# Contexts of later batches turned by VectorE and kept turned in DRAM, in a fused cross-attention and expert kernel

## The chip, the cores and the metric

The kernel runs on one core of a Trainium2 chip. A core has five engines with queues of their own: TensorE (PE in the profile; its weight loads are shown apart as PEld), VectorE (DVE), ScalarE (ACT), GpSimd (POOL) and SyncE (SP), which here only issues transfers. The time is device microseconds of one execution, and the median over runs counts.

## The reference

Two layers follow each other, all in float32. The first is a gated cross-attention: `x` (4 batches, 256 rows, 512 columns) gives the queries, `ctx_4096` (4 batches, 1601 rows, 512 columns) the keys and values. There are 32 query heads of 128 columns, 8 key and value heads, so that four query heads share one. The second is a router with low-rank experts.

```python
q = (query @ Wq + bq).reshape(B, L, NKV, G, HDIM)
k_, v_ = jnp.split(kv @ Wkv + bkv, 2, axis=-1)
...
scores = jnp.einsum('blkgd,bmkd->bkglm', q, k) * scale
attn = jax.nn.softmax(scores, axis=-1)
o = jnp.einsum('bkglm,bmkd->blkgd', attn, v).reshape(B, L, NHEAD * HDIM)
...
x = x + jnp.tanh(g_xattn[0]) * attention(layernorm(x), ctx_4096, ...)
x = x + jnp.tanh(g_ffn[0]) * experts(layernorm(x), ...)
```

## The kernel before

**Groups.** Batch b, key head h and half l of the 256 query rows make a group; there are 64, in this order. In group sc_h_l of a batch `run_group` interleaves the score matmuls of the group (L1142, tiles `sc`) with the value products of the group before it (L1233, tiles `av`). Scores are copied to `p` by ACT (L1151), their maximum is folded by DVE as they come (L1067 to L1073), spread over the partitions by a short chain that ends with a transpose of 32x32 blocks into `mb` (L1086 to L1107, then L1100), and then subtracted from `p` tile by tile (L1181, DVE), exponentiated (L1184, ACT), and summed (again L1067 to L1073, tiles `sm`). `p` is a ring of buffers: a score tile of a later group waits for the sum of the tile that held its buffer.

**Filler.** The rest of PE's work is cut into tasks and put between the groups and between the steps of a group: query, key and value projections of coming heads (L896 for keys and queries, L907 for values), the output projection (L1310), and the turning of contexts.

**Contexts.** A batch's context is needed with its 512 columns on the partitions (`ctxT`, 4 chunks of 128 columns by 1602 places), as an operand of the projections. It comes in 13 tiles of 128 rows, the last of 65. `ctx_steps` loads a tile into one of two `stage` buffers; `turn_ctx` has PE turn it by four transposes (L258, tile `pt_ctx`), which ACT copies out of PSUM (L260). For batch 0 half of the copies are DVE's. For batches 1 to 3 all this is a task of one step to a tile, which runs in group sc_6_1 of the batch before, once the last value projection of that batch (V pair 3) has used the old context: there is one `ctxT`.

**Projections by seven products.** Keys, values and queries are computed two heads at a time with seven products in place of eight, from blocks of the operands: the context as two column halves by two row halves (b11, b12, b21, b22), and sums of them. The sums of the context are T1 = b12 - b11, T2 = b22 - T1, T4 = b21 - T2 (`ctx_sums`, L723, tile `T`), done here for each pair of tiles by pieces of 128 columns, and, once all are done, b12 := b22 - b12 in place in `ctxT` (`last_sums`, L734, in two pieces of 417 and 384 columns, then L738 for the 65 remaining rows). The products of a pair run in the order 1 (b11), 2 (b21), 6 (T2), 7 (b12), 5 (T1), 4 (T4), 3 (b22), by column pieces of 417 and 384. Product 7 needs the b12 of L734. ACT copies and DVE adds (L941, L951) bring the products into `kT`.

**At a boundary of batches.** The order is: V pair 3 of the old batch; group sc_6_1 with the turning; group sc_7_0; then K pair 0 of the new batch (tiles `pxk`, `pzk`, `pyk`), whose first step is `last_sums`; and after it V pair 0 and group sc_7_1. Weights for the next pairs are loaded and summed ahead, and kept in DRAM for the other batches.

**Order of the work.** The order of PE, DVE and ACT is that in which the program issues it; the program holds a clock of its own for each engine. `later` puts a piece of DVE or ACT work in a named queue with its planned length and the time or the key that it needs, `pump` issues from the queue whose head can start first, and `force(key)` issues what is needed until the key is done. A plan's LAG is the time from a load's issue at which the piece that needs it may be planned. The order of SP and POOL is the scheduler's. Each engine works strictly in its order, and a transfer issued from SP waits in SP's queue for what it needs.

Of the kernel before, what the change touches and what calls it, by code (L numbers as in the profile page):

```python
# [10 lines left out]
F32 = mybir.dt.float32  # L11
# [4 lines left out]
P = 128  # L16
# [11 lines left out]
def flamingo_kernel(  # L28
# [93 lines left out]
    clock = {"now": 0.0, "v": 0.0, "a": 0.0, "hold": 0.0}  # L122
    free = [0.0] * NBANK
    done = {}
    queues = {q: deque() for q in ("sub", "oT", "so", "exp", "ln", "T", "norm", "sum", "low", "low_a")}

    def vec(ns, ready=None):

# [41 lines left out]
    def force(key):  # L170


        while key not in done:
            q = next((q for q in queues.values() if any(p[4] == key for p in q)), None)
            if q is None:

                assert pump(most=1), key
                continue
            ready = q[0][2]
            if not isinstance(ready, float):  # L180
                force(ready)

            engine, start = q[0][0], start_of(q[0])
            for name, other in queues.items():
                fit = 1200 if name == "sub" else FIT
                while other is not q and other and other[0][0] == engine:
                    if start_of(other[0]) + other[0][1] > start + fit:
                        break
                    take(other)
            take(q)  # L190
        return done[key]
# [390 lines left out]
        xa_t[b] = pool.tile([P, NL, D], F32, tag=f"xa{b}", name=f"xa_{b}", bufs=1)  # L582
    STAGE = 2

    LAG_DMA, LAG_CTX, LAG_X = 2500, 1700, 3000


    JOINT = 2
# [60 lines left out]
    def ctx_col(i):  # L649

        half, t = divmod(i, HK // P)
        return half * HW + HT + t * P
# [5 lines left out]
    def new_ctx(b):  # L658
        ctxT_t[b] = pool.tile([P, NC, 2 * HW], F32, tag="ctxT", name=f"ctxT_{b}", bufs=1)
        rest_t[b] = pool.tile([P, NC, REST], F32, tag="rest", name=f"rest_{b}", bufs=1)  # L660
        if REST0 < HT:

            nc.gpsimd.memset(ctxT_t[b][:, :, REST0:HT], 0.0)

    def ctx_steps(b):

        staged = {}

        def load(n):
            i = ctx_order[n]  # L670
            s = pool.tile([P, D], F32, tag="stage", name=f"ctx_{b}_{i}", bufs=STAGE)
            nc.sync.dma_start(s[: rows[i]], ctx_kv[b, i * P : i * P + rows[i], :])
            staged[i] = s

        def begin():
            new_ctx(b)
            new_sums(b)

        def step(n):
            def run():  # L680
                i = ctx_order[n]
                if n + STAGE - 1 < KT:
                    load(n + STAGE - 1)
                turn_ctx(b, i, staged.pop(i))
                if n % 2 == 1 and i < FULL:
                    ctx_sums(b, ctx_col(i) - HW, P)
                if i == FULL:
                    ctx_sums(b, 0, HT)
                if n == KT - 1:
                    done["ctx", b] = clock["now"] + 1000  # L690
            return NC * TR_COST, LAG_CTX, run, True

        def first():
            for n in range(STAGE - 1):
                load(n)


        return [(0, 0, first), (0, ("pair", "v", b - 1, NKV // 2 - 1), begin)] + [
            step(n) for n in range(KT)
        ]  # L700

    def new_sums(b):
        t = pool.tile([P, 6 * HW + 2 * REST], F32, tag="T", name=f"T_{b}", bufs=1)
        T_t[b] = (
            t[:, : 6 * HW].rearrange("p (n c k) -> p n c k", n=3, c=2),
            t[:, 6 * HW :].rearrange("p (c k) -> p c k", c=2),
        )

    def ctx_sums(b, s0, n):


        ct, T = ctxT_t[b], T_t[b][0]
        lo, hi = slice(s0, s0 + n), slice(HW + s0, HW + s0 + n)
        b11, b12, b21, b22 = ct[:, 0:2, lo], ct[:, 0:2, hi], ct[:, 2:4, lo], ct[:, 2:4, hi]
        t1, t2, t4 = T[:, 0, :, lo], T[:, 1, :, lo], T[:, 2, :, lo]
        for out_, x_, y_ in (
            (t1, b12, b11),
            (t2, b22, t1),
            (t4, b21, t2),
        ):  # L720
            later(
                "T", "v", 80 + 2.3 * n, clock["now"] + 1000.0,
                lambda o=out_, x=x_, y=y_: nc.vector.tensor_tensor(o, x, y, ALU.subtract),  # L723
            )

# [16 lines left out]
    def turn_ctx(b, i, src):  # L742
        if i < FULL:
            lo = ctx_col(i)
            transpose_rows(
                src, P, ctxT_t[b][:, :, lo : lo + P], f"ctx_{b}_{i}", b > 0 or i % 2 == 1
            )
            return

        rest = rest_t[b]  # L750
        transpose_rows(src, REST, rest, f"ctx_{b}_{i}", True)
        nc.scalar.copy(ctxT_t[b][:, :, :REST0], rest[:, :, :REST0])
        act(300)
        nc.scalar.copy(ctxT_t[b][:, :, HW : HW + HT], rest[:, :, REST0:])
        act(300)
# [925 lines left out]
    def run_group(cur, prev, ahead=AHEAD, most=NC * TR_COST):  # L1681


        for j in range(NPAIR + ahead):
            if cur is not None and j < NPAIR:
                score_unit(cur, j)
                if j == NPAIR - 1 and cur[0] == B - 1 and cur[1] >= NKV - 2:
                    softmax(cur)
                short_tasks(most)
            if prev is not None and prev[2] == 0 and j > 2:  # L1690
                block_sums(prev, j >= NPAIR - 1)
            if prev is not None and j >= ahead:
                av_unit(prev, j - ahead)
                short_tasks(most)
        if cur is not None and not (cur[0] == B - 1 and cur[1] >= NKV - 2):
            softmax(cur)
# [173 lines left out]
    for hi, (b, h) in enumerate(heads):  # L1870
        pair, coming = (b, h // 2), next_pair(b, h // 2)
        nxt = heads[hi + 1] if hi + 1 < len(heads) else None
        for l in range(NL):
            now = hi * NL + l
            cur = (b, h, l)
            if cur == last:
                break
            if (h, l) == (NKV - 5, 1) and b + 1 < B and (b + 1) % JOINT == 0:
                load_pair("q", b + 1, 0)
                tasks.append(Task(x_steps(b + 1), now + 7))  # L1880
            run_group(cur, prev)
            if prev is not None:
                steps = out_steps(prev)
                if steps:
                    tasks.insert(0, Task(steps, now + 1 if by_blocks(*prev[:2]) else None))
                    if by_blocks(*prev[:2]):
                        out_task[prev[:2]] = tasks[0]
            prev = cur
            if (b, h, l) == (B - 1, NKV - 3, NL - 1):
                flush(lambda t: t in out_task.values())  # L1890
                tail_space()
                tasks.append(Task(ffn_weight_steps() + [(0, 0, early_norms)]))
                both = [ffn_steps(*t) for t in early]
                tasks[:0] = [Task(route, now + 4) for route, _ in both]
                tasks.extend(Task(steps, spare=True) for _, steps in both)
            if nxt is not None and nxt[0] % JOINT == 0:
                tasks.append(Task(q_steps(*nxt, l), now, first=True))
            elif nxt is not None and l == 0:
                load_q(*nxt)
            if coming is not None and (h % 2, l) == (0, 1):  # L1900
                cb, cp = coming
                if cb == b:
                    then = lambda c=coming: next_weights("v", *c)
                    steps = sum(pair_steps("k", cb, cp, then), [])
                else:
                    steps = first_k_steps(cb)
                tasks.append(Task(steps, (hi | 1) * NL + (NL - 1) * (cb == b), now))
            if coming is not None and (h % 2, l) == (1, 0):
                cb, cp = coming
                follow = next_pair(cb, cp)  # L1910
                then = None if follow is None else lambda f=follow: next_weights("k", *f)
                for part in pair_steps("v", cb, cp, then):
                    tasks.append(Task(part, (hi | 1) * NL + NL, now))
                if cb == b and cp == NKV // 2 - 1 and b + 1 < B:
                    tasks.append(Task(ctx_steps(b + 1)))
            if (h, l) == (NKV - 1, NL - 1) and b + 1 < B:

                force(("T", "kv", b + 1))
                force(("w", "v", b + 1, 0))
            window(now)  # L1920
            if l == NL - 1 and nxt == heads[-1]:
                load_wo(*nxt)
# [51 lines left out]
```

## Time and profile before

| what | value |
|---|---|
| median of 3 runs (lowest to highest) | 2558.49 us (2557.35 to 2559.09) |
| span of the profiled execution | 2555.5 us |
| granted TensorE clock | 1.00 of full speed throughout |
| PE busy on L1142 and L1233, scores and value products | 775.9 and 766.1 us |
| PE busy on `pt_ctx` (L258), 208 transposes, batch 0's among them | 273 ns median of one |
| ACT copies of `pt_ctx` (L260) to `ctxT`, 42 | 589 ns median of one |
| DVE subtraction L1181 (128x1024) and exponential L1184 | 1137 and 990 ns mean |
| DVE sums L723: 128x256, 128x66, 128x834, 128x768 | 54, 9, 3 and 3 of them |
| transfers | 167.16 MB, mean 65 GB/s |

The span is that of one execution of the program, taken by the hardware profiler; the runs' times hold some 3 us around it. A row of the profile's groups gives a line of the kernel, the engine, the operation with its output and input tiles, the number of instructions, and their time. In a timeline the columns are start, length, engine, line, operation, tiles and number. Matmuls are pipelined, so that the lengths of neighbouring PE rows overlap a little: the distance from start to start is what a row costs.

### The profile page before, as it was taken

To read this page: it belongs to the slowest core of one execution; us is meant where nothing else is said; L and a number is where in the kernel's file an instruction comes from. 1 tells how busy PE (TensorE), PEld (TensorE's weight loads), DVE (VectorE), ACT (ScalarE), POOL (GpSimd) and SP (SyncE) were. 2 spreads that over 40 slices of the span, in tenths; PEclk is the share of its full clock that TensorE was granted. 3 is DMA by queue.
4 is the path that set the end of the run, shared out by engine and by line. 5 is a ranking of instruction groups with operands and counts; after the bars stand their busy time and mean duration, and the time that the engine had idled before them with its cause. 6 is when DMAs were issued, how large, how long until landed. Compare 5 with 4: busy or idle time off the path is not lost.

```text
span 2555.5 us, 26175 instructions
## 1 busy us (share of the span) xinstructions
PE 2547.3 (100%) x9235; PEld 1487.8 (58%) x9235; DVE 2202.6 (86%) x3310; ACT 1188.1 (46%) x1897; POOL 150.4 (6%) x401
## 2 busy tenths in 40 slices
PE   9999999999999999999999999999999999999999
PEld 7557566565555656455565665756656455555554
DVE  4889898899889989899788887878889899998897
ACT  3544454445434555455444444445454445544551
POOL 0000000000000000110000000000000000000000
PEclk9999999999999999999999999999999999999999
DMA  4313222324110111012121111212221011111000
GB/s 158 123 64 108 87 95 84 114 85 149 48 56 23 44 52 56 25 40 83 49 81 37 62 52 62 81 48 81 85 84 56 25 52 52 52 44 52 17 17 33
DMA packets 75499, 167.16 MB, mean 65 GB/s; under 512 B 5372, under 2 KB 32028, under 8 KB 72808
## 3 DMA queue, kind: packets, MB, share of 16 engines
q1 hardware_dynamic: 74424, 164.41, 19.3%
q8 instruction: 73, 1.20, 0.2%
q0 software_dynamic: 416, 0.81, 0.1%
q14 instruction: 58, 0.48, 0.1%
q10 hardware_dynamic: 528, 0.26, 0.0%
HBM read 119.06 MB, written 46.40 MB: 65 GB/s over the span
## 4 chain that ended last, share of the span: by engine, by line
PE 99%; DVE 1%; DMA 0%; ACT 0%; issue 0%; DVEq 0%; ACTq 0%
PE av L1233 28%; PE sc L1142 28%; PE pxk L896 6%; PE pxv L907 6%; PE pxq L896 4%; PE pyk L896 3%; PE pyv L907 3%; PE po L1310 3%; PE pox L484 3%; PE pyq L896 2%; PE pzk L896 2%; PE pzv L907 2%; PE poy L484 1%; PE pzq L896 1%; PE ptv L1020 1%; PE pk L803 1%
## 5 line engine op out<-in xcount | busy, mean ns | idle before, releaser
L1142 PE MATMUL sc<-qT,kT 128*128 128x512 f32 (+1 forms) x1664 | 775.9, 592 | 0.0
L1151 ACT COPY p<-sc 65x512 f32<-65x512 f32 x820 | 474.3, 586 | 636.5 <-PE sc L1142 575.2
L1233 PE MATMUL av<-p,v 65*128 65x512 f32 x1640 | 766.1, 592 | 1.2 <-ACT p L1184 1.2
L1233 PEld LDWEIGHTS av<-p,v 65*128 65x128 f32 x1640 | 309.5, 190 | 376.2 <-issue 370.8
L1142 PEld LDWEIGHTS sc<-qT,kT 128*128 128x128 f32 (+1 forms) x1664 | 307.0, 186 | 374.3 <-issue 340.4
L1181 DVE TENSOR_TENSOR p<-p,mb 65x512 f32<-65x512 f32 x442 | 485.9, 1137 | 0.1
L1184 ACT ACTIVATE p<-p 65x512 f32<-65x512 f32 x442 | 423.1, 990 | 38.6 <-DVE p L1181 34.5
L1073 DVE TENSOR_TENSOR mx<-mx,p 128x1024 f32<-128x1024 f32 x252 | 308.1, 1223 | 137.9 <-ACT p L1151 134.8
L1073 DVE TENSOR_TENSOR sm<-sm,p 128x1024 f32<-128x1024 f32 x252 | 307.4, 1220 | 9.8
L1090 POOL COPY quad_sm<-quad_sm 32x16 f32<-32x16 f32 x186 | 70.7, 380 | 2088.3 <-DVE quad_sm L1086 2083.1
L896 PE MATMUL pxq<-xq,wq 128*128 128x256 f32 x512 | 131.2, 379 | 0.0
L941 ACT ACTIVATE kT<-pxk,biasT 128x384 f32<-128x384 f32 (+1 forms) x120 | 57.9, 508 | 141.8 <-PE pxk L896 141.0
L896 PEld LDWEIGHTS pxq<-xq,wq 128*128 128x128 f32 x512 | 92.5, 189 | 31.2 <-issue 15.3
L941 ACT ACTIVATE qT<-pxq,biasT 128x256 f32<-128x256 f32 x64 | 30.3, 473 | 140.2 <-PE pxq L896 140.2
L944 ACT COPY v<-pxv 128x384 f32<-128x384 f32 x90 | 43.0, 477 | 104.8 <-PE pxv L907 104.8
L896 PE MATMUL pxk<-T,wk 128*128 128x417 f32 (+1 forms) x240 | 90.4, 499 | 0.0
L907 PE MATMUL pxv<-wv,T 128*128 128x128 f32 x720 | 90.2, 275 | 0.0
L896 PE MATMUL pxk<-ctxT,wk 128*128 128x417 f32 (+1 forms) x240 | 90.0, 499 | 0.0
L907 PE MATMUL pxv<-wv,ctxT 128*128 128x128 f32 x720 | 90.0, 275 | 0.0
L907 PEld LDWEIGHTS pxv<-wv,T 128*128 128x128 f32 x720 | 86.4, 192 | 4.7 <-issue 4.3
L907 PEld LDWEIGHTS pxv<-wv,ctxT 128*128 128x128 f32 x720 | 86.4, 192 | 4.7 <-issue 4.3
L1067 DVE TENSOR_TENSOR mx<-p,p 128x1024 f32<-128x1024 f32 x63 | 76.8, 1220 | 13.1 <-ACT p L1151 12.8
(264 smaller groups left out, 2809.6 us busy)
## 6 DMA issues: line engine op xcount, KB each, us to landing
wo<-in_L_xattn_Wo_dram SPq DMA_DIRECT2D x18, 1024.0 KB, 5.3
kept_q<-wq SPq DMA_DIRECT2D x16, 896.0 KB, 4.8
wq<-kept_q SPq DMA_DIRECT2D x16, 896.0 KB, 5.1
wo<-kept_wo SPq DMA_DIRECT2D x13, 1024.0 KB, 5.8
wk<-kept_k SPq DMA_DIRECT2D x11, 896.0 KB, 4.6
wv<-kept_v SPq DMA_DIRECT2D x11, 896.0 KB, 4.4
ctx<-in_ctx_dram SPq DMA_DIRECT2D x36, 256.0 KB, 2.7
wq<-in_L_xattn_Wq_dram SPq DMA_DIRECT2D x32, 256.0 KB, 3.1
```

The source lines that it names most:

```text
L484: nc.tensor.matmul(bk[:, :HD], left[i]()[:, c, :], blk[:, c, :], start=first and c == 0, stop=c == 1, skip_group_check=True,)
L896: nc.tensor.matmul(bk[:, :n], a(SLOT[i], c), operand(i, c, s, n), start=first and c == 0, stop=c == 1, skip_group_check=True,)
L907: nc.tensor.matmul(bk[:, t * HDIM : (t + 1) * HDIM], operand(i, c, s + t * P, P), a(SLOT[i], c), start=first and t == 0 and c == 0, stop=c ...
L941: nc.scalar.activation(dst, src, AF.Identity, bias=bias_of(kind, h0 + f))
L1067: nc.vector.tensor_tensor(acc, p[first], p[first + 1], op)
L1073: nc.vector.tensor_tensor(acc, acc, p[j], op)
L1142: nc.tensor.matmul(sc[:r, :], kT_t[b, h][:, key_col(i) : key_col(i) + r], qT_t[b, h][:, :, l * P : (l + 1) * P], start=True, stop=True,)
L1151: nc.scalar.copy(p[:r, k, :], sc[:r, :])
L1181: nc.vector.tensor_tensor(p, p, m, ALU.subtract)
L1184: nc.scalar.activation(p, p, AF.Exp, scale=scale)
L1233: nc.tensor.matmul(av, v_t[b, h][:r, i, :], p_t[key][j][:r, k, :], start=(j == 0 and k == 0), stop=(j == NPAIR - 1 and k == len(pairs[j]) ...
L1310: nc.tensor.matmul(po, oT_t[key][:, g, :], w_t["o", b, h][:, g, :], start=(g == 0), stop=(g == G - 1),)
```

## The change

**Turning.** `ctx_steps` no longer loads and turns. In each of the first twelve groups of batches 0 to 2, ahead of `run_group`, `swap_ctx` handles one tile of the next batch's context (two in the twelfth): SP loads it into a `stage` buffer; DVE transposes its 32x32 blocks (up to sixteen along the columns, for four bands of 32 rows) into the other `stage` buffer, as a piece of a new queue "turn"; SP stores each band of 32 rows, 64 KB, in a DRAM tile of 512 columns by 1602 places, in runs of 32 elements (128 bytes). A tile must be stored before the next one is begun. The last tile's row 1600 is left out of this. Only batch 0 is still turned by PE.

**Reloading.** When V pair 3 of the old batch is done, `begin` asks for the kept context to be complete, makes the new `ctxT`, and reloads it by eight transfers, four of 768 KB and four of 32 KB, and two for `rest`, the tile of the last 65 rows, all on SP. Row 1600 comes by two transfers of 512 single elements on POOL.

**Sums.** The T sums of the context are now six instructions, by the two column pieces of 417 and 384 instead of seven narrower pieces. They are planned 24 us (LAG_CTX) after the reload's issue, and so is `last_sums`, which is forced by K pair 0's first step as before. In the order that the program issues, the three sums of the first piece come among the maxima of group sc_7_0 (at the second boundary the third of them later), and those of the second piece and `last_sums` between and behind that group's subtractions L1181. At the first two boundaries the output projection `po_6_0` now stands ahead of the first K product on PE. PE has 39 rows of four transposes less, DVE 39 block transposes more and 45 sums fewer, ACT 36 copies of 128x512 fewer and those of the last tiles.

```diff
-    LAG_DMA, LAG_CTX, LAG_X = 2500, 1700, 3000
+    LAG_DMA, LAG_CTX, LAG_X = 2500, 24000, 3000
...
+    def swap_ctx(b, n):
+
+        i = ctx_order[n]
+        if n:
+            force(("kept", b, n - 1))
+        if b not in ctx_kept:
+            ctx_kept[b] = dram.tile([D, 2 * HW], F32, tag=f"ctx_{b}", name=f"kept_ctx_{b}")
+        kept_b = ctx_kept[b].rearrange("(j k) w -> k j w", k=32)
+        r = rows[i] // 32 * 32
+        src = pool.tile([P, D], F32, tag="stage", name=f"ctx_{b}_{i}", bufs=STAGE)
+        nc.sync.dma_start(src[:r], ctx_kv[b, i * P : i * P + r, :])
+        dst = pool.tile([P, D], F32, tag="stage", name=f"swap_{b}_{i}", bufs=STAGE)
+
+        def swap():
+            nc.vector.transpose(dst[:r], src[:r])
+
+        def store():
+            for a in range(r // 32):
+                if i < FULL:
+                    lo = ctx_col(i) + 32 * a
+                else:
+                    lo = HW * a
+                nc.sync.dma_start(
+                    kept_b[:, :, lo : lo + 32],
+                    dst[32 * a : 32 * a + 32].rearrange("k (j w) -> k j w", w=32),
+                )
+
+        later("turn", "v", 710, clock["now"] + LAG_DMA, swap, ("swap", b, n))
+        later("turn", "v", 0, ("swap", b, n), store, ("kept", b, n))
+
     def ctx_steps(b):
...
         def begin():
+            force(("kept", b, KT - 1))
             new_ctx(b)
             new_sums(b)
-
-        def step(n):
-            def run():
-                i = ctx_order[n]
-                if n + STAGE - 1 < KT:
-                    load(n + STAGE - 1)
-                turn_ctx(b, i, staged.pop(i))
-                if n % 2 == 1 and i < FULL:
-                    ctx_sums(b, ctx_col(i) - HW, P)
-                if i == FULL:
-                    ctx_sums(b, 0, HT)
-                if n == KT - 1:
-                    done["ctx", b] = clock["now"] + 1000
-            return NC * TR_COST, LAG_CTX, run, True
...
+            ends = [(0, HT, HW), (1, HT, HW), (0, 0, 32), (1, 0, 32)]
+            for c in range(0, NC, 2):
+                for half, lo, hi in ends:
+                    lo, hi = half * HW + lo, half * HW + hi
+                    nc.sync.dma_start(ct[:, c : c + 2, lo:hi], kept_b[:, c : c + 2, lo:hi])
+            for half in range(2):
+                nc.sync.dma_start(
+                    rest[:, :, 32 * half : 32 * half + 32], kept_b[:, :, HW * half : HW * half + 32]
+                )
+            one = ctx_kv[b, LK - 1, :].rearrange("(c p) -> p c", p=P)
+            nc.gpsimd.dma_start(rest[:, :, REST - 1], one)
+            nc.gpsimd.dma_start(ct[:, :, HW + HT - 1], one)
+            done["ctx", b] = clock["now"] + LAG_CTX
+            for s0, n in parts_of_half:
+                ctx_sums(b, s0, n, LAG_CTX)
+
+        return [(0, ("pair", "v", b - 1, NKV // 2 - 1), begin)]
...
-    def ctx_sums(b, s0, n):
+    def ctx_sums(b, s0, n, lag=1000.0):
...
-                "T", "v", 80 + 2.3 * n, clock["now"] + 1000.0,
+                "T", "v", 80 + 2.3 * n, clock["now"] + lag,
...
+            if b + 1 < B and now % (NKV * NL) < KT - 1:
+                for n in range(KT)[now % (NKV * NL) :][: 1 if now % (NKV * NL) < KT - 2 else 2]:
+                    swap_ctx(b + 1, n)
             run_group(cur, prev)
```

More of the change, by code (lines that the diff above doesn't have):

```diff
@@ L124, in flamingo_kernel @@
     done = {}
-    queues = {q: deque() for q in ("sub", "oT", "so", "exp", "ln", "T", "norm", "sum", "low", "low_a")}
+    queues = {q: deque() for q in ("sub", "oT", "so", "exp", "ln", "T", "norm", "sum", "turn", "low", "low_a")}
     def vec(ns, ready=None):
@@ L663, in new_ctx @@
             nc.gpsimd.memset(ctxT_t[b][:, :, REST0:HT], 0.0)
-    def ctx_steps(b):
-        staged = {}
-        def load(n):
-            i = ctx_order[n]
-            s = pool.tile([P, D], F32, tag="stage", name=f"ctx_{b}_{i}", bufs=STAGE)
-            nc.sync.dma_start(s[: rows[i]], ctx_kv[b, i * P : i * P + rows[i], :])
-            staged[i] = s
+    ctx_kept = {}
+    def swap_ctx(b, n):
[23 more added lines that the diff above has]
+        later("turn", "v", 0, ("swap", b, n), store, ("kept", b, n))
@@ L675, in begin @@
+    def ctx_steps(b):
         def begin():
+            force(("kept", b, KT - 1))
             new_ctx(b)
             new_sums(b)
-        def step(n):
-            def run():
-                i = ctx_order[n]
-                if n + STAGE - 1 < KT:
-                    load(n + STAGE - 1)
-                turn_ctx(b, i, staged.pop(i))
-                if n % 2 == 1 and i < FULL:
-                    ctx_sums(b, ctx_col(i) - HW, P)
-                if i == FULL:
-                    ctx_sums(b, 0, HT)
-                if n == KT - 1:
-                    done["ctx", b] = clock["now"] + 1000
-            return NC * TR_COST, LAG_CTX, run, True
@@ L693, in first @@
[L693 to L700, printed above, removed]
+            ct, rest = ctxT_t[b], rest_t[b]
+            kept_b = ctx_kept[b].rearrange("(c p) w -> p c w", p=P)
+            spare = rows[FULL] % 32
+            whole = rows[FULL] - spare
+            assert spare == 1 and whole == 64 and REST0 == 32
+            ends = [(0, HT, HW), (1, HT, HW), (0, 0, 32), (1, 0, 32)]
@@ L745, in turn_ctx @@
             transpose_rows(
-                src, P, ctxT_t[b][:, :, lo : lo + P], f"ctx_{b}_{i}", b > 0 or i % 2 == 1
+                src, P, ctxT_t[b][:, :, lo : lo + P], f"ctx_{b}_{i}", i % 2 == 1
             )
```

## The prediction, made before the changed kernel ran

> **What bounds the kernel now.** I read the shares of busy time, the chain of waits, PE's waits, then the timelines at the change. The page first:
>
> ```profile
> PE 2547.3 (100%) x9235; PEld 1487.8 (58%) x9235; DVE 2202.6 (86%) x3310; ACT 1188.1 (46%) x1897; POOL 150.4 (6%) x401
> ...
> PE 99%; DVE 1%; DMA 0%; ACT 0%; issue 0%; DVEq 0%; ACTq 0%
> ```
>
> TensorE (PE) is 99% of the chain that ends last: a microsecond taken from it is won, unless PE then waits. Its waits by releaser:
>
> ```profile
> PE av L1233 <- ACT p L1184: 1.2, 1, 1.2
> PE warm L1795 <- DVE ones L1792: 1.1, 1, 1.1
> ```
>
> Nothing longer exists, and the 1.2 lies at 1195.3 us, late in batch 1. VectorE (DVE) is the next bound. Its share by stretch (length, PE, PEld, DVE busy):
>
> ```profile
> 741.00:947.00 206.00, 206.00 (x673) 112.19 (x672) 182.59 (x269) 97.45 (x153) 10.64 (x36) 1.00 0.14 48
> 1058.00:1127.00 69.00, 69.00 (x230) 36.68 (x230) 63.81 (x87) 33.68 (x51) 12.59 (x12) 1.00 0.11 35
> 1127.00:1196.00 69.00, 68.29 (x273) 38.26 (x271) 65.21 (x100) 33.09 (x58) 11.06 (x19) 1.00 0.23 73
> ```
>
> DVE has 11% spare early in batch 1, but only 5.2 us in 69 from 1058 on, just before that wait.
>
> **What it removes.** PE's timeline in the group (sc_6_1 of batch 0) where batch 1's contexts are turned; columns are start, length, engine, line:
>
> ```profile
> 583.61 1.88 PE L1142 MATMUL sc<-qT,kT 128*128 128x512 f32 x4
> 585.33 0.60 PE L258 MATMUL pt_ctx<-ident,ctx 128*128 128x128 f32 x4
> 585.77 1.88 PE L1233 MATMUL av<-p,v 128*128 128x512 f32 x4
> ```
>
> Score matmuls start 2.16 us before av matmuls here; without transposes, at 621.38 and 623.09, 1.71. A tile's four transposes cost 0.44. The 65-row tile costs 0.25 (1192.30 to 1192.55). 12 x 0.437 + 0.25 = 5.5 us for each later batch, 16.5 in all. ACT loses 36 copies of 0.59 us and some small ones, 24 us: at 46% busy it gains PE nothing.
>
> **What it adds, hidden.** 39 VectorE transposes. The same shape exists:
>
> ```profile
> L1107 DVE STREAM_TRANSPOSE mx<-mx x64: 711/711/712, 75.4 to 2477.3; 128x512 f32<-128x512 f32 x64
> ```
>
> 39 x 0.71 = 28 us of DVE at most (25 by the 0.64 from start to start of successors). The 63 narrow sums (36+18 of 0.42, 9 of 0.24, 25 us) become 18 wide ones of 1.03 and 0.95 (18 us). DVE thus gains about 20 us of work over 2555, thinly spread, a transpose or two in a group of 39 us. Between an exp's end and its av matmul I read mostly 7 to 24 us: that covers one transpose. Without it each would cost 0.64 to 0.71, 28 in all. A transpose also waits for its tile's load; behind it in DVE's order stand the subtractions L1181 of the running group, for which ACT's exp and then PE's av matmuls wait. The load is issued a group earlier (39 us) and lands in 2.7 us, so the wait should be nothing, except where two transposes stand close together (below).
>
> DMAs: 39 loads as before, now a batch earlier, 150 stores of 64 KB, 24 reloads (12 of 768 KB, 12 of 32 KB), 6 rest pieces, 6 GpSimd gathers of 512 single elements; POOL's memset stays. Rows:
>
> ```profile
> wq<-kept_q SPq DMA_DIRECT2D x16, 896.0 KB, 5.1
> ctx<-in_ctx_dram SPq DMA_DIRECT2D x36, 256.0 KB, 2.7
> ffn_w<-in_L_ffn_lora_A_dram POOLq DMA_DIRECT2D x4, 64.0 KB, 2.9
> ```
>
> A reload, 3.3 MB, takes 18 us at 896 KB per 5.1 us (some 180 GB/s), 27 with the weights queued beside it. It is issued at the end of the last V pair (577 us for batch 1), first needed by a DVE sum near 624: 47 us against 27. No cost; each microsecond beyond costs one, behind it on DVE the maxima. No 128-byte run is in the trace; lora_A's run is 64 bytes, 1024 of them landing in 2.9 us, so a store of 512 runs should take 1.5 to 2.9. SP issues cost 0.33 to 0.5 us: four stores 2 us a group. But they wait for the transpose in SP's queue with weight loads behind them: a late transpose delays those. Loads run pairs ahead, so I take 0, bound 0 to 3 us a batch.
>
> A rule against the change: the Trainium skill, "VectorE: DVE Perf Modes", section "The three transpose paths", warns that a plain copy which transposes by strides runs 19 times slower than the crossbar. Were the stores that bad (19 x 2.7 us = 51 a tile), estimated from that page, they would overrun the 39 us group and the context come late by over 100 us a batch. The blocks are already turned and runs are 128 bytes, so I follow the lora_A row, 2.9. No run here shows the rule's case.
>
> **What moves onto the path.** Before, the T sums are spread over the group of the transposes and finish early:
>
> ```profile
> 629.54 1.02 DVE L734 TENSOR_TENSOR ctxT<-ctxT 128x834 f32<-128x834 f32 x1
> ...
> 633.35 0.95 DVE L734 TENSOR_TENSOR ctxT<-ctxT 128x768 f32<-128x768 f32 x1
> ...
> 643.03 0.71 DVE L1100 STREAM_TRANSPOSE mb<-quadm_mx 128x512 f32<-128x512 f32 x1
> ```
>
> PE takes them up much later, in the first K product:
>
> ```profile
> 640.26 1.56 PE L896 MATMUL pxk<-ctxT,wk 128*128 128x417 f32 x4
> 641.66 1.56 PE L896 MATMUL pzk<-ctxT,wk 128*128 128x417 f32 x4
> 643.06 1.56 PE L896 MATMUL pxk<-T,wk 128*128 128x417 f32 x4
> 644.46 1.56 PE L896 MATMUL pyk<-ctxT,wk 128*128 128x417 f32 x4
> ```
>
> In the new order the second-piece T sums and L734's subtraction (which changes ctxT in place) come behind mb, between the subtractions L1181 of group 7_0. The third product's second half waits for T2's second piece, the fourth product for L734. Everything before is 5.5 us earlier. Behind the waiting PE stand the remaining K products and the next group; nothing else fills PE.
>
> - Batch 0 to 1: mb ends at 643.7 - 5.5 - 0.5 (the old last sums leave, less what T1 adds) = 637.7. Then DVE does a po addition 0.7, a 65-row subtraction 0.57, three of 1.14, three sums of 0.95, L734 1.02: 8.6, ends 646.3 to 646.6. PE reaches the fourth product at 644.5 - 5.5 + 3.4 (po_6_0 now stands ahead) = 642.4. Stall 4 to 4.3.
> - 1 to 2: mb 1220.5 - 5.5 + 0.6 = 1215.6 (PE comes to the wait above 5.5 us earlier, DVE only about 5, so 1.2 becomes 1.8). Behind it three q additions 1.2, all seven subtractions 7.4, po 0.7, a sum of 1.03, three of 0.95, L734: 14.2, ends 1229.8. PE: 1226.6 - 5.5 + 0.6 + 3.4 = 1225.1. Stall 4.7.
> - 2 to 3: mb 1887.1 - 5.5 - 0.6 = 1881.0, then 0.57 + 3 x 1.14 + 3 x 0.95 + 1.02 = 7.9, ends 1888.9. PE: 1887.7 - 5.5 = 1882.2, no po to cover. Stall 6.4 to 6.7.
>
> Sum 15.6, bounds 8 (DVE ahead of this walk by 2.5 a boundary) to 22 (behind by 2). Not in the trace: how far DVE slips late in batch 1. There three transposes, two of them one behind the other with a wait for the first one's four stores (issue 4 x 0.43 + landing 2.9 = 4.7, less 2.3 of work between, 2.4), and one more table-load pair on ACT (1.28) meet 5.2 us of spare. Bounds 0 and 8 (all of it comes on PE through score copies that find no buffer); the nearest row is the single 1.2 wait, so I take 2.5.
>
> **Sum.** The profiled execution spans 2555.5, the median of the runs is 2558.5, 3.0 around it. 2555.5 + 3.0 - 16.5 + 15.6 + 2.5 = 2560.1. I say 2560.
>
> **Rivals.**
> - A, the gain stays: the sums come before PE needs them and batch 1 holds. 2558.5 - 16.5 = 2542 if no stall; with the lower 8, 2550. For it: PE idles nowhere today, slacks of 7 to 24 us let DVE run ahead. Against it: the order behind mb is fixed, and mb is bound to PE's own last scores.
> - B, forecast: given back at three K starts, 2552 to 2566.
> - C, slower: DVE becomes the bound in batch 1 from 1058 us. It decides once three transposes and the 2.4 wait exceed 5.2 us of spare and the maxima's buffers run out; then 8 there, K stalls at 17 to 22, plus 2 or more for late weights: 2558.5 - 16.5 + 8 + 17 to 22 + 2 = 2569 to 2574. For it: 94% busy and the 1.2 wait. Against: the narrow sums leave sc_6_1, which gives DVE 8 us back right after.
> - D, transfers: a store or reload held in SP's queue past the 20 us to spare. 5 us late at each boundary: 2575. Against: DMA share 0.11 to 0.29.
>
> **Chances.** B 0.45, A 0.27, C 0.22, D 0.06. From B's spread of 2552 to 2566, within 0.2% (about what a measurement of this kernel tells from no change, 5.1 us, 2553.4 to 2563.6) is 0.30, faster 0.04, slower 0.11; A gives faster 0.25, same 0.02; C and D slower. Faster 0.29, same 0.32, slower 0.39. The range takes in most of A and C: 2546 to 2574; B alone 2552 to 2566.
>
> **What would show it.** PE without L258 for batches 1 to 3; three PE waits of 4 to 6.5 us at the fourth K product, released by DVE's in-place ctxT subtraction; a wait near 1100 to 1196. Waits released by DMA would speak for D. No such waits, and a span near 2539, for A. Many small waits spread over batches 0 to 2 would make this wrong: then the transposes themselves were not hidden.

## The result, and the profile after

| | before | after |
|---|---|---|
| median of the runs | 2558.38 us (2557.35 to 2559.09, 4 runs) | 2593.39 us (2592.76 to 2593.92, 4 runs) |
| span of the profiled execution | 2555.5 us | 2591.0 us |
| PE's idle gaps over 0.3 us, added up | 2.85 us | 43.65 us |
| matmul lengths above the usual one of their kind, added up | 0.4 us | 11.6 us |

The ratio is 1.0139, with a 95% interval of 1.0124 to 1.0153: slower by 35 us, where 2560 with a range of 2546 to 2574 was forecast. The account closes: -16.5 for the transposes, +40.8 for new gaps, +11.2 for slow matmuls make 35.5, the difference of the spans. The last two rows of the table are worked out from the trace, row by row of PE, without the first microseconds of the program. A run's time holds 1.8 us around its span here (2592.76 against 2591.0 us), not some 3.

The page of the changed kernel, shares of busy time and the chain of waits:

```profile
PE 2541.7 (98%) x9079; PEld 1476.3 (57%) x9079; DVE 2221.6 (86%) x3304; ACT 1167.2 (45%) x1854; POOL 174.0 (7%) x407
...
PE 94%; DVE 4%; issue 1%; DMA 1%; ACT 0%; SPq 0%; DVEq 0%; ACTq 0%
```

PE has 156 matmul records fewer, yet only 5.6 us less busy time, and VectorE now holds 4% of the chain. PE's waits by releaser:

```profile
PE pxk L920 <- ACT kT L965: 29.6, 3, 12.9
PE sc L1166 <- ACT p L1175: 9.2, 1, 9.2
PE av L1257 <- ACT p L1208: 2.6, 2, 1.7
```

Three waits at the K starts, as forecast, but twice as long, released by ACT and not by VectorE. PE's timeline at the first boundary:

```profile
638.58 1.56 PE L920 MATMUL pxk<-ctxT,wk 128*128 128x417 f32 x4
639.98 1.56 PE L920 MATMUL pzk<-ctxT,wk 128*128 128x417 f32 x4
652.07 3.15 PE L920 MATMUL pxk<-T,wk 128*128 128x417 f32 x4 [10.53 <-ACT kT L965]
655.01 2.38 PE L920 MATMUL pyk<-ctxT,wk 128*128 128x417 f32 x4
```

The wait is at the third product, not at the fourth. The third product adds into the same PSUM bank `pxk` as the first, so it needs ACT to have copied the first one out. ACT and DVE there:

```profile
650.31 1.06 ACT L1208 ACTIVATE p<-p 128x1024 f32<-128x1024 f32 x1 [0.95 <-DVE p L1205]
651.27 0.74 ACT L965 ACTIVATE kT<-pxk,biasT 128x384 f32<-128x384 f32 x2
```

```profile
644.05 0.95 DVE L747 TENSOR_TENSOR T<-ctxT,T 128x768 f32<-128x768 f32 x1
644.92 1.22 DVE L1205 TENSOR_TENSOR p<-p,mb 128x1024 f32<-128x1024 f32 x1
646.06 1.02 DVE L758 TENSOR_TENSOR ctxT<-ctxT 128x834 f32<-128x834 f32 x1
```

The first product was ready to be copied at 640. ACT copied it at 651.27, behind six exponentials (seven at the second boundary, six at the third), each of which waited for its subtraction, and between the subtractions stand the T sums and the in-place subtraction. The context itself was ready in time: the reloads landed 16 to 20 us after their issue (576.9 to 592.9, 1176.4 to 1196.0, 1845.9 to 1862.2), and the first sum ran some 30 us behind that at every boundary (at 624.29 at the first).

The slow products behind the wait (2.94 us from start to start for the third, 2.22 for the fourth, 1.40 before) go with a lower granted clock. The stretch from 650 to 665 us of the changed kernel (length, then busy time of PE, PEld, DVE, ACT and POOL, then the clock):

```profile
650.00:665.00 15.00, 12.93 (x32) 7.05 (x33) 13.14 (x22) 5.79 (x10) 3.50 (x6) 0.78 0.00 1
```

The 9.2 us lie late in batch 1. DVE stands for a tile's load between two subtractions. ACT's next exponentials wait for those subtractions, ACT's copies of the scores stand behind the exponentials, and so PE's scores find no free bank:

```profile
1102.26 0.71 DVE L681 STREAM_TRANSPOSE swap<-ctx 128x512 f32<-128x512 f32 x1 [5.52 <-DMA ctx<-in_ctx_dram]
```

```profile
1107.07 2.08 PE L1166 MATMUL sc<-qT,kT 128*128 128x512 f32 x2 [9.15 <-ACT p L1175]
```

The load had been issued at 1096.57, after the transpose of the tile before and its four stores, and took 5.4 us. Such a stand came once in each of the three batches, where two transposes stand within 10 us of each other: 3.6, 5.5 and 1.2 us. PE waited behind the one of 5.5 alone. The transfers' rows:

```profile
kept_ctx<-swap SPq DMA_DIRECT2D x150, 64.0 KB, 5.0
ctx<-in_ctx_dram SPq DMA_DIRECT2D x36, 256.0 KB, 5.4
```

### The profile page after: what moved, and what is told of

The parts are those of the page before. It is cut to its first block, busy times and chain, and to the rows that moved or that the text cites. A ratio compares the mean times of both kernels' runs of the same rounds, so it can differ in the third digit from the quotient of the medians.

```text
span 2591.0 us, 26129 instructions
## 1 busy us (share of the span) xinstructions
PE 2541.7 (98%) x9079; PEld 1476.3 (57%) x9079; DVE 2221.6 (86%) x3304; ACT 1167.2 (45%) x1854; POOL 174.0 (7%) x407
## 4 chain that ended last, share of the span: by engine, by line
PE 94%; DVE 4%; issue 1%; DMA 1%; ACT 0%; SPq 0%; DVEq 0%; ACTq 0%
PE sc L1166 26%; PE av L1257 26%; PE pxk L920 6%; PE pxv L931 6%; PE pxq L920 4%; PE pyv L931 3%; PE pyk L920 3%; PE po L1334 3%; PE pox L484 3%; PE pyq L920 2%; PE pzv L931 1%; PE pzk L920 1%; PE poy L484 1%; DVE p L1205 1%; PE pzq L920 1%; PE ptv L1044 1%
## 5 line engine op out<-in xcount | busy, mean ns | idle before, releaser
L1114 POOL COPY quad_sm<-quad_sm 32x16 f32<-32x16 f32 x186 | 76.5, 411 | 2105.3 <-DVE quad_sm L1110 2100.1
L920 PE MATMUL pxk<-T,wk 128*128 128x417 f32 (+1 forms) x240 | 95.2, 520 | 29.6 <-ACT kT L965 29.6
L1121 POOL COPY quadm_sm<-quadm_sm 32x16 f32<-32x16 f32 x186 | 84.6, 455 | 169.0 <-DVE quadm_sm L1233 163.8
```

The costliest lines, as they stand in the source:

```text
L920: nc.tensor.matmul(bk[:, :n], a(SLOT[i], c), operand(i, c, s, n), start=first and c == 0, stop=c == 1, skip_group_check=True,)
L1121: eng.tensor_copy(m[32 * a : 32 * a + 32], m[:32])
```

## The experiments

Each is set beside the changed kernel (2593.4 us) or the kernel before, whose runs beside them took 2557.4 to 2557.9 in the median. Spans and waits are of the profiled execution.

### ACT's copy ahead of the exponentials

`copied` holds when the first product of a K start has been copied; an exponential of group 7_0 becomes ready when its subtraction and that copy are issued.

```diff
                     done[key] = done[nm, s, "x0"] = copy_to(0, 0, s, n, bk)
+                    if is_k and hp == 0 and b > 0 and b not in copied:
+                        copied[b] = done[key]
...
-            later("exp", "a", 1060 if n > 1 else 630, ("sub", key, j), exp, ("exp", key, j))
+            go = ("go" if holds(key) else "sub", key, j)
+            later("exp", "a", 1060 if n > 1 else 630, go, exp, ("exp", key, j))
```

> The changed kernel (2593.4 us) with one edit to ACT's order alone: the copy of the first K product out of PSUM is issued ahead of the exponentials of group 7_0, instead of behind six or seven of them; the orders of PE and DVE stay. Theory (the long K-start waits of 10.5, 6.2 and 12.9 us come of ACT: the copy that the third product needs stands behind exponentials whose subtractions stand among the late T sums): the wait moves to the fourth product, is released by DVE's in-place subtraction of ctxT, and is 4 to 5, 4 to 5 and 6 to 7 us, as walked in the prediction; 29.6 becomes about 16, and the time 2576 to 2580. Rival (DVE's late sums alone set the end of the wait, whatever ACT does): waits and time as in the changed kernel, 2593.

Measured: 2589.3 us (2588.8 to 2589.8, 2 runs). PE at the first boundary:

```profile
641.71 0.86 PE L931 MATMUL pxk<-T,wk 128*128 128x417 f32 x2
643.38 0.97 PE L931 MATMUL pxk<-T,wk 128*128 128x417 f32 x2 [0.81 <-DVE T L758]
647.46 3.15 PE L931 MATMUL pyk<-ctxT,wk 128*128 128x417 f32 x4 [3.11 <-DVE ctxT L769]
...
657.46 2.96 PE L931 MATMUL pxk<-ctxT,wk 128*128 128x417 f32 x8 [3.22 <-DVE kT L986]
```

The third product's second half waits for T2 and the fourth for the in-place subtraction, as the prediction walked: 3.9, 4.5 and 6.3 us at the three boundaries, 14.7 in all (15.6 walked). So ACT's order made 15 of the 29.6 us at these products. But the time was missed by 10 us. Over half of what ACT gave came back at the last product of the piece: it waits for DVE's addition to `kT`, which stands behind the subtractions and sums, 3.2, 1.1 and 4.0 us. And with two or three gaps to a boundary in place of one, 2.6 us more of slow matmuls came. Of the K starts' 29.6 us of waiting 23 remain: moving ACT's copy alone does not mend them.

### The sums early

```diff
-    LAG_DMA, LAG_CTX, LAG_X = 2500, 24000, 3000
+    LAG_DMA, LAG_CTX, LAG_X = 2500, 14000, 3000
```

> The changed kernel with LAG_CTX 14000 in place of 24000, so that the T sums are issued some ten microseconds earlier, ahead of group 7_0's maxima, and the in-place subtraction mostly among them. Theory: the reload has landed by then (16 to 20 us after its issue), no K start waits over 2 us, and the clock stays full there: 2593.4 - 29.6 - 7 = 2557, with the 9.2 us wait of batch 1 still in it. Rival (the reload is late for them and DVE waits for transfers, with the maxima behind): waits of DVE on the reload of 3 us and more at each boundary, 2570 or above.

Measured: 2566.8 us (2565.6 to 2569.4, 4 runs), ratio to before 1.0037 (1.0018 to 1.0057). The first sum ran at 595.34 instead of 624.29, no transfer held it, and the K start behind batch 0 has no wait. The rows:

```profile
PE sc L1166 <- ACT p L1175: 9.9, 1, 9.9
PE pxk L920 <- ACT kT L965: 6.9, 2, 4.8
```

27 us come back when the sums are issued earlier, of a gross loss of 52 (the 35 measured and the 16.5 taken from PE). Waits of 2.1 and 4.8 us remain at the other two K starts, where the in-place subtraction still came late (1889.87 for its second piece at the third). The expectation held the wait of batch 1 already and was missed by 10 us: these two waits make 6.9 of them, slow matmuls that stayed 1.5, and two waits in batch 1 that grew (9.2 to 9.9, 1.7 to 2.4) the rest.

### Wide sums alone

The kernel before with TensorE's turning, and nothing else of the change.

```diff
-                if n % 2 == 1 and i < FULL:
-                    ctx_sums(b, ctx_col(i) - HW, P)
-                if i == FULL:
-                    ctx_sums(b, 0, HT)
                 if n == KT - 1:
+                    for s0, m in parts_of_half:
+                        ctx_sums(b, s0, m)
```

> The kernel before (2558), contexts turned by TensorE as there, with one part of the change alone: the T sums as six wide instructions to a batch, issued behind the last turned tile instead of pair by pair. In DVE's order the sums of the second piece and the in-place subtraction then stand behind mb, between the subtractions of group 7_0, and in ACT's order four, seven and seven exponentials stand ahead of the copy of the first K product. Theory (the order of the sums makes the K-start waits, whoever turns the contexts): waits of 5 to 13 us at the three K starts, 20 to 30 in all, and slow products behind each: 2558 + 25 + 6 = 2589, at least 2575. Rival (the waits come of what the transposes on VectorE, the stores and the reload do): no K start waits over 2 us, 2556 to 2560.

Measured: 2587.9 us (2587.8 and 2587.9, 2 runs), ratio 1.0120 (1.0099 to 1.0140).

```profile
PE pxk L894 <- ACT kT L939: 23.8, 3, 11.2
```

With nothing moved from TensorE to VectorE, no store and no reload, the K starts wait 6.5, 6.1 and 11.2 us and 7 us of slow matmuls follow. So the order of the sums is shown to be the cause of the waits at the K starts: late sums bring them without any of the rest of the change, and earlier sums (the experiment before) take most of them away with all the rest in place. They need no turning on VectorE and no reload. What brings them from the 23.8 here to the 29.6 of the changed kernel was not taken apart.

### The wait filled with matmuls

```diff
+                if i == 2 and is_k and hp == 0 and b > 0 and s == parts0:
+                    for _ in range((22, 12, 27)[b - 1]):
+                        nc.tensor.matmul(bk, ident, ctxT_t[b][:, 0, :512], start=True, stop=True)
                 product(i, s, n, bk, i in (1, 2, 7))
```

> The changed kernel with 22, 12 and 27 matmuls of 128x128 by 512 put ahead of the second K product at the three boundaries (9.4, 5.2 and 11.6 us at 0.43 each); their result is overwritten. Theory (an idle TensorE is granted a lower clock for some microseconds after it): the waits shrink by what was put in, to about 1 us each, the third and fourth products take 1.40 us again instead of 2.9 and up to 2.8, and the time falls by 7, to 2586. Rival (the slow products come of something else, contention or the weight loads): the products stay slow and the time stays 2593.

Measured: 2607.1 us (2 runs). The filling was mis-sized: one such matmul of the program is two of 0.43 us in the trace, so that 52.4 us were put in for 29.6 of waiting.

```profile
639.60 19.04 PE L996 MATMUL pzk<-ctxT,ident 128*128 128x512 f32 x44
...
659.88 1.56 PE L920 MATMUL pxk<-T,wk 128*128 128x417 f32 x4
661.28 1.56 PE L920 MATMUL pyk<-ctxT,wk 128*128 128x417 f32 x4
```

The question is answered all the same: without the gap the third and fourth products take 1.40 us from start to start (the next row starts at 662.68). The span grew by 13.7, not by 52.4 - 29.6 = 22.8, and the other 9.1 are slow matmuls that went: some 7.5 behind the three gaps, and 1.8 behind the gap of 1.7 late in batch 1, which is still there (1217.59) but this time had no slow matmul behind it.

### The transpose later

```diff
-        later("turn", "v", 710, clock["now"] + LAG_DMA, swap, ("swap", b, n))
+        later("turn", "v", 710, clock["now"] + 12000.0, swap, ("swap", b, n))
```

> The changed kernel with VectorE's block transpose planned 12 us after its load in place of 2.5. In batch 1 the transpose of tile 11 then stands eight instructions behind that of tile 5, not two. Theory (the 9.2 us wait of PE at 1098 us comes of DVE standing 5.5 us at that transpose for its load): that wait goes, with the slow matmuls behind it (1.9) and the 0.9 before it: 2593.4 - 12 = 2581.5. Rival (DVE is saturated there and PE waits anyway): 5 us or more of the wait remain, 2586 or above.

Measured: 2588.1 us (2 runs). DVE no longer stands for the load, and the wait falls from 9.15 to 4.77 us:

```profile
1102.13 2.08 PE L1166 MATMUL sc<-qT,kT 128*128 128x512 f32 x2 [4.77 <-DVE oT L1316]
```

Half of it was the load; the rest is what the rival named. ACT's copies of the scores wait for buffers `p` that DVE has not summed yet, because its sums stand behind all seven subtractions.

### No block transposes

```diff
-        dst = pool.tile([P, D], F32, tag="stage", name=f"swap_{b}_{i}", bufs=STAGE)
+        dst = src
...
-            nc.vector.transpose(dst[:r], src[:r])
+            pass
```

> The changed kernel without VectorE's 39 block transposes: each tile is loaded and stored as it came, in the same runs of 128 bytes. (The contexts of batches 1 to 3 are thereby not turned; this part of the computation is left out.) Theory: of the changed kernel's loss only the wait in batch 1 hangs on the transposes, through the stand for the load (5.5 us) and their own 28 us of DVE's time: the 9.2 us wait and its slow matmuls go, the three K-start waits stay at 29.6 or a little less: 2593.4 - 12 = 2581. Rival (DVE's load is what makes all of it late): the K waits shrink too, by a third or more, below 2570.

Measured: 2593.4 us (2592.4 and 2594.3, 2 runs), against 2581 expected.

```profile
PE pxk L920 <- ACT kT L965: 29.6, 3, 12.9
PE pyq L920 <- ACT qs_q L965: 5.0, 1, 5.0
...
PE sc L1166 <- ACT p L1175: 2.4, 1, 2.4
```

The K-start waits are the same 29.6 to the tenth, so VectorE's 28 us of transposes have no part in them. The wait of batch 1 fell from 9.15 to 2.36. That gain of 7 was lost again at 65.9 us, where a new wait of 5.0 with 3 us of slow matmuls behind it appears: ACT stands there until a store from its own buffer (`qs_q` to `kept_q`) has landed, and stores of contexts, which no longer wait for a transpose, go out beside it. Their share in that wait was not tried by itself.

### The edits together

Three runs put edits together. The first gives two tiles to a group (the second begun in the middle of it) up to the seventh group, in all batches, with the sums early and ACT's copy first. The second does so in batch 1 alone, with one tile to a group in the others, the sums early and ACT's copy where it was. The third is the second with ACT's copy first. The lines below are those of the second of the three runs; `midway` holds a tile that `run_group` begins in the middle of the group.

```diff
-            if b + 1 < B and now % (NKV * NL) < KT - 1:
-                for n in range(KT)[now % (NKV * NL) :][: 1 if now % (NKV * NL) < KT - 2 else 2]:
-                    swap_ctx(b + 1, n)
+            if b == 1 and now % (NKV * NL) < 7:
+                n = 2 * (now % (NKV * NL))
+                swap_ctx(b + 1, n)
+                if n + 1 < KT:
+                    midway.append(lambda b=b, n=n: swap_ctx(b + 1, n + 1))
+            elif b != 1 and b + 1 < B and now % (NKV * NL) < KT:
+                swap_ctx(b + 1, now % (NKV * NL))
```

> The changed kernel with three edits: LAG_CTX 14000 (sums early), ACT's copy of the first K product ahead of group 7_0's exponentials, and two tiles in each of the first six groups of a batch and one in the seventh (the second begun in the middle of the group), so that no transpose stands late in batch 1; transposes planned 6 us after their loads. Theory: no K start waits over 2 us, the wait of batch 1 is gone, PE keeps its gain of 16.5 us less 2 to 5 of small waits: 2543 to 2549, faster than both kernels. Rival (VectorE is too full in batch 1 whatever the place of the transposes, or two tiles to a group make DVE stand for loads): waits of 8 us or more remain, 2553 or above.

Measured: 2571.8 us (2569.2 to 2574.0, 4 runs), ratio 1.0060 (1.0043 to 1.0076). A miss: with two tiles to every early group DVE stood ten times for a load or a store, 16.1 us in all, the waits of PE were spread over the batches, and those at 1102.8 and 1201.9 us stayed at 3.5 and 2.5.

> The changed kernel with LAG_CTX 14000, transposes planned 12 us after their loads, and in batch 1 alone two tiles to each of the first six groups and one in the seventh, so that its transposes end where VectorE still has room; batches 0 and 2 keep one tile to a group, thirteen groups. Theory (batch 1's long wait comes of transposes that stand where VectorE has no room, the loss of the combined kernel before this one of loads that were late for two tiles to a group): the wait of 9.9 us in batch 1 is gone or under 2 us, the K starts keep 2.1 and 4.8 us; 2566.8 - 9.9 - 0.9 - 2 = 2554. Rival (VectorE lags in batch 1 through the work it has all over, and moving transposes within it changes nothing): 5 us or more of the wait stay, 2560 or above.

Measured: 2561.7 us (2558.7 to 2564.7, 10 runs), ratio 1.0015 (1.0006 to 1.0024). The best of the changed orders, and still not faster than before. DVE waits for no tile, but PE waits 3.5 us near 1095 although no transpose is left within 100 us of it: ACT's copy of the scores stands behind five exponentials there and then waits for a sum on DVE. Waits of 2.5, 2.1 and 4.8 follow, and 5.8 us of slow matmuls stand behind the four.

> The kernel of the run before with ACT's copy of the first K product ahead of group 7_0's exponentials as well. Theory: the waits of 2.1 and 4.8 us at the second and third K start shrink to what VectorE's additions leave, 1 to 3 us each: 2 to 4 us less than the run before, 2550 to 2552, faster than both kernels. Rival (the wait only moves from ACT's copy to VectorE's addition, product by product): the same time as the run before, within 1 us.

Measured: 2563.8 us (2561.2 to 2567.4, 10 runs), ratio 1.0026 (1.0016 to 1.0035). The rival is right on the waits, which went from ACT's copy to DVE's additions (2.5 and 2.7 us, and 2.0 at ACT). The time is 2.1 us above the run before, not within 1. In the profiled execution the slow matmuls and a wait of 2.5 us at the program's first context load, which the edit does not touch, make it longer; whether they make the 2.1 us in the other runs is not shown.

### How much there was to gain

```diff
-        for c in range(NC):
-            nc.tensor.transpose(pt[:, c, :n], src[:n, c * P : (c + 1) * P], ident[:n, :n])
+        if name.startswith("ctx") and not name.startswith("ctx_0") and n == P:
+            pt = src.rearrange("p (c k) -> p c k", k=P)
+        else:
+            for c in range(NC):
+                nc.tensor.transpose(pt[:, c, :n], src[:n, c * P : (c + 1) * P], ident[:n, :n])
```

> The kernel before, its orders of ACT, DVE and transfers unchanged, with TensorE's transposes of the 36 full tiles of batches 1 to 3 taken out and nothing in their place; ACT copies the loaded tile as it is. (The contexts of these batches are thereby not turned; this part of the computation is left out.) It asks how much of the 15.7 us that these transposes cost on TensorE (36 x 0.437) can be had at all. Theory (late in batch 1 VectorE has no room, and TensorE coming 5.2 us earlier runs into it): a new wait of 3 to 4 us near 1090 us, where an exponential ended 1.8 us before its use, the wait of 1.2 us near 1195 grows, slow matmuls follow each: 2557.5 - 15.7 + 3.4 + 1.5 + 3 = 2550. Rival (TensorE is the only bound, and all of it can be had): 2541 to 2543, with no new waits.

Measured: 2550.4 us (2549.0 to 2553.4, 8 runs), ratio 0.9971 (0.9961 to 0.9982).

```profile
PE pxq L899 <- ACT qT L944: 4.4, 2, 3.2
PE av L1236 <- ACT p L1187: 2.7, 1, 2.7
```

Of 15.7 us taken from PE, with nothing put anywhere else, 7.5 arrive in the median. The profiled execution is the slowest of the eight, 3 us above it: there 3.9 arrive, and the rest goes into waits of 4.4 and 2.7 (1.2 before) and 5.7 us of slow matmuls. The size was foreseen, one place not: no wait appeared near 1090; it came at 608.7. There the query projection waits for ACT's copies, and these stand behind ACT's copies of context tiles, which wait for their loads (19.7 us over the program, none before):

```profile
607.68 0.62 ACT L263 COPY ctxT<-ctx 128x512 f32<-128x512 f32 x1 [2.25 <-DMA ctx<-in_ctx_dram]
```

In the changed kernel ACT copies no context there. So the 4.4 us, and the slow matmuls behind them, belong to this run and not to the change; the wait of 2.7 at 1193.3 does not hang on these loads.

## Why the prediction was wrong

- *What bounds the kernel*, and *what it removes*: right, 16.5 us off PE. But it took the whole of it as won but for the moved sums and 2.5 us late in batch 1. Taken out alone (15.7 of it) it brought 7.5, some of the rest being lost to loads that this run alone has; how much of the 16.5 the other engines' orders would have let through in the changed kernel is not shown.
- *VectorE's transposes hidden*: right in size (0.70 us each) and right for batches 0 and 2, where no wait of PE hangs on them.
- *Transfers*: the reload is hidden, as forecast. The store was put at 1.5 to 2.9 us and took 5.0 (2.4 to 9.5), and the loads took 5.4 instead of 2.7. Where two transposes stand close together, DVE stood three times for such a load, 10.4 us in all, and the stand of 5.5 reached PE.
- *What moves onto the path*, the step that failed. It says that "the third product's second half waits for T2's second piece, the fourth product for L734". Of the third product's inputs it walked the sums on VectorE and left out the PSUM bank that it adds into: that had to be copied by ACT first, and ACT's order had six or seven exponentials ahead of the copy, each behind its subtraction. The walk of VectorE was right for these two products (14.7 measured against 15.6 once ACT's copy was moved), but it also ended too early: DVE's additions to `kT`, behind the same sums, then held the last product for 8.3 more. The wait was 29.6, and 23.8 with the wide sums alone.
- *Late in batch 1*: the mechanism was named with the right buffers, at 2.5 of a bound of 8. It measured 9.2: DVE stood 5.5 us for the load where 2.4 were walked, which is about half (4.8 remain when the transpose is later), and the sums behind the subtractions did the rest.
- *What the sum leaves out*: the price of a gap beyond its length. 11.2 us of slow matmuls stand behind the gaps; no term had them; added to the other terms as they were walked they give 2571.
- *Rivals*: C had the place in batch 1 and K starts at 17 to 22, and ended at 2574 for want of the same two terms. A and D did not come; the sums were early enough only when they were issued early.

The wait of 3.5 us in batch 1 that is left when its transposes are done early was not taken apart further: it may come of PE's earlier arrival, of the 9 us of transposes before it, or of both.

## What to carry to other kernels

For an instruction that will wait, walk every one of its inputs, the accumulator's bank among them, and for each the queue ahead of it on the engine that provides it: an engine at 45% can hold the path by its order alone. Merging small pieces of off-path work into large ones saves their time, but where the large ones wait for the last of their input it loses the early start; here that cost 30 us where it saved 7 on an engine that was not the bound. In this kernel a gap of 3.5 us or more on TensorE cost its length and 1.7 to 3.3 us more in slow matmuls; a shorter one, from 1.7 us up, cost that in some executions and nothing in others.

## What the runs showed of the hardware

Behind a gap of PE its matmuls can run slow for a few microseconds. In the changed kernel, lengths above the usual one sum to 1.8 us behind a gap of 1.71, 2.0 behind 9.15, 2.6 behind 10.53, 3.3 behind 6.19 and 1.7 behind 12.91, and to 3.6 behind a gap of 2.67 in the run without turning. Behind gaps of 0.86 and 1.20 us no matmul was over 0.15 us longer. The rows at the smallest of these gaps with slow matmuls:

```profile
1211.56 1.13 PE L1257 MATMUL av<-p,v 65*128 65x512 f32 x2 [1.71 <-ACT p L1208]
1212.52 3.12 PE L1166 MATMUL sc<-qT,kT 128*128 128x512 f32 x4
1215.44 2.38 PE L1257 MATMUL av<-p,v 128*128 128x512 f32 x4
```

Four score matmuls take 2.92 us from start to start here, 1.72 elsewhere, and the granted clock is 0.50 from 1213.0 to 1216.4 us. But a short gap does not always do this: the gap of 1.70 us at the same place in the runs with ACT's copy first and with the wait filled had no slow matmul behind it and a clock of 1.00, nor had one of 2.11 us with the sums early or one of 3.22 with ACT's copy first. In all the runs together, slow matmuls stand behind every gap of 3.47 us and over, behind some from 1.70 to 3.24, and behind none under that past the program's start. What decides between them was not tried.

The Trainium skill, "TensorE: Matmul & The Clock Gate", section "Why this matters for your kernels", asks for no idle gaps over about 3 us between bursts of matmuls, since the clock then falls to half. The trace agrees on the half (clock 0.50 from 646.5 to 656.5 us, and 2.94 us in place of 1.40 behind 10.53). On the length it agrees for the longer gaps, but 1.71 us could already be enough, and there the trace decides.

Stores of 64 KB in runs of 128 bytes landed in 5.0 us in the median, 13 GB/s each. The 256 KB loads of contexts, as a rule issued just behind four such stores, took 5.4 us where they had taken 2.7 without them. Whether the stores slow the loads was not tried by itself.
